# A decoder layer on one Trainium2 core: the routed experts' upper parts in seven block products (Strassen, f32)

## The chip, the cores and the metric

The kernel is one program on one core of a Trainium2 chip. TensorE (PE in the profile, with its weight loads as PEld), VectorE (DVE), ScalarE (ACT), GpSimd (POOL) and SyncE (SP, which here only issues transfers) run their own instruction streams and wait for each other by semaphores. The metric is the device time of one execution in microseconds; a kernel's time is the median of its runs.

## The reference, cut to what matters

The input `x` is 4 x 512 tokens of width 512, in f32. Three sublayers are added to it, each on a layer-normalised copy: causal attention with 32 query and 8 key heads of width 64; a product with a context matrix, both sides rounded block by block to an 8-bit float format; and a mixture of experts. In the last, which the change is about, each token goes to the expert of its highest router score, at most 256 tokens to one expert, and a shared expert takes all tokens:

```python
xd = jnp.zeros((E * C, d), x.dtype).at[flat].set(xt, mode='drop')
xd = xd.reshape(E, C, d)                       # E = 8, C = 256, d = 512
h = jax.nn.silu(jnp.einsum('ecd,edh->ech', xd, W1)) * jnp.einsum('ecd,edh->ech', xd, W3)   # h = 704
oe = jnp.einsum('ech,ehd->ecd', h, W2).reshape(E * C, d)
out = jnp.take(oe, jnp.minimum(flat, E * C - 1), axis=0)
out = out * (gate * keep.astype(x.dtype))[:, None]
shared = jax.nn.silu(xt @ sw1) * (xt @ sw3) @ sw2
return (out + shared).reshape(b, sl, d)
```

The kernel computes these products in f32.

## The kernel before, in words

**Stages.** The attention stage goes through 80 steps written out by hand (`steps`), each with scores, transposes of the probabilities and weighted sums of two or three units. Between them a filler (`Fill.upto`) puts in pieces of other work, kept as generators (`job_q`, `job_k`, `job_v`, `job_o`, the layer norms, the quantised product `job_t`, the router `job_w`). Each job is added with a step from which it may start, a cost in PE time and the jobs that it needs; a job that needs VectorE or GpSimd waits until the filler's own count of GpSimd time (`work.gpsimd`, raised by the helper `gpsimd`) allows it. The result is a fixed order of instructions on every engine. The filler's counts decide places only; they are not hardware.

**Router.** `job_w(b)` normalises block b (512 tokens), computes router scores and places, and scatters the rows to `xd` with four indirect transfers from GpSimd, each waiting for the one before.

**Shared expert.** When the steps are done, `units` take over: `shared_up(b, c)` computes chunk c (128 of the 704 hidden columns) of the upper part for block b, and `shared_down(b, j)` the down product for two tiles of 128 tokens. Between pieces of a unit, `between` lets the filler finish its jobs. A chunk's plain form (`up`) is eight PE products, four over the depth for W1 and four for W3, then Silu on ScalarE and a product on VectorE; the sixth chunk is half W1, half W3 (64 columns each). In blocks 1 to 3 the five full chunks are done by `up7` instead: W1's and W3's columns, stacked, times the block's tokens are one product of a 2 x 2 block matrix with a 2 x 2 block matrix (split by depth and by token half), and Strassen's scheme in Winograd's form needs seven block products for it in place of eight. Each has half the token columns and half the depth, so two PE products. The seven need sums of weight blocks (`weight_sums`, four GpSimd operations a chunk, into `wS` and partly in place) and of token blocks (`token_sums`, four GpSimd operations a block, into `xSs`). The seven results, in PSUM banks, are added up as they come: `p1` and `p5` are copied out by ScalarE, `u2` and `u3` made by VectorE, two more sums (`u2 + p5`, `c2`) by GpSimd, the rest by VectorE; at last GpSimd multiplies the gated half `g` by `c2`.

**Banks.** PSUM banks go by tag: four `sp`, one `av`, three `mm`. `up7` takes six from `sp` and `p5`'s from `av`; the down products of the experts use `mm`.

**Routed experts.** After the jobs, for each of eight experts: `load_rows` brings its 256 rows, `turn_rows` transposes them, `expert_up` calls the plain `up` with 256 columns for six chunks, `down` multiplies by W2, and the rows go to `oe`. The gated chunks lie in what was `wS` (two halves, one for each parity of e). The weights of expert e + 2 take the slot of expert e (`slots[e % 2]`): `load_e(e + 2)` is called after expert e's down product and issues W1, W3 and W2 from SP. The order on PE of one turn of the loop is: chunks 1 and 2 of e, transposes of e + 1, chunks 3 to 5, chunk 0 of e + 1, the down product of e.

**End.** In the last turn `rows_back` brings back 16 tiles of partial results (shared part and residual), ten of them into buffers no longer needed: block 3's `h3x`, `xSs` and the free half of `wS`. Three shared down products are kept for last; beside them GpSimd gathers the experts' rows (16 indirect transfers), VectorE scales and adds them, SP stores the result.

Of the kernel before, what the change touches and what calls it, by code (L numbers as in the profile page):

```python
# [23 lines left out]
def decoder_layer(  # L24
# [18 lines left out]
    nc = tc.nc  # L43
    B, T, D = x.shape
    HD = 64
    NQ = wq.shape[1] // HD
    E, _, H = W1.shape
# [224 lines left out]
    def gpsimd(us, *args):  # L272
        nc.gpsimd.tensor_tensor(*args)  # L273
        work.gpsimd = max(work.gpsimd, work.at) + 1000 * us
# [469 lines left out]
    def add(due, cost, key, gen, *after, want=None):  # L744

        jobs.append(Job(due, cost, key, gen, after, want))

    MM4 = 4 * 860
    for b in range(B):
# [58 lines left out]
        for j in range(TB):  # L808
# [4 lines left out]
        add(ze + 5, 4 * 440 + 4000, ("w", b), job_w(b), *[(("t", b, j), 1) for j in range(TB)], *([(("cs", b + 1), 0)] if b < B - 1 else []))  # L813
    add(8, 0, ("zero",), job_zero())
    jobs.sort(key=lambda x: x.rank())
    for key in [("h", 0)]:
# [267 lines left out]
    def load_ffn(slot, w1, w3, w2, issue, cuts=(0, H)):  # L1084

        v13 = slot[:, 0 : 2 * KC * H].rearrange("p (k h) -> p k h", k=KC)
        v2 = slot[:, 2 * KC * H :].rearrange("p (c d) -> p c d", c=NHC)
        w1r, w3r = (w.rearrange("(k p) h -> p k h", p=P) for w in (w1, w3))  # L1090
        for lo, hi in zip(cuts, cuts[1:]):
            issue(out=v13[:, :, lo:hi], in_=w1r[:, :, lo:hi])
            yield v13, v2
            top = min(hi, H - HT)
            issue(out=v13[:, :, H + HT + lo : H + HT + top], in_=w3r[:, :, lo:top])
            if hi == H:
                issue(out=v13[:, :, H : H + HT], in_=w3r[:, :, top:H])
# [134 lines left out]

    T2 = T // 2
    wS = gp.tile([P, 3, 2, HF * P], F32, name="wS")
    xSs = gp.tile([P, 4, 2, T2], F32, name="xS")
    xS = {}

    def blocks(c):  # L1240

        w, cols = se["w"][0], slice(c * P, (c + 1) * P)
        low = slice(H + HT + c * P, H + HT + (c + 1) * P)
        return w[:, 0:2, cols], w[:, 2:4, cols], w[:, 0:2, low], w[:, 2:4, low]

    def weight_sums(c):

        a11, a12, a21, a22 = blocks(c)
        s2, s3, s4 = (wS[:, i, :, c * P : (c + 1) * P] for i in range(3))
# [5 lines left out]
    def token_sums(b):  # L1255

        x = h3x[b]
        b11, b12, b21, b22 = (x[:, k : k + 2, t : t + T2] for k in (0, 2) for t in (0, T2))
        t1, t2, t3, t4 = (xSs[:, i] for i in range(4))
        gpsimd(1.27, t1, b12, b11, ALU.subtract)  # L1260
        gpsimd(1.27, t3, b22, b12, ALU.subtract)
        gpsimd(1.27, t2, b22, t1, ALU.subtract)
        gpsimd(1.27, t4, b21, t2, ALU.subtract)
        xS[b] = t1, t2, t3, t4, b11, b21, b22

    def up7(b, c, mid):
        a11, a12, s1, a22 = blocks(c)
        s2, s3, s4 = (wS[:, i, :, c * P : (c + 1) * P] for i in range(3))
        t1, t2, t3, t4, b11, b21, b22 = xS[b]

        def product(i, w, x):
            ps = bank("av" if i == 3 else "sp", f"p7_{b}_{c}_{i}")[:, 0:T2]
            for k in range(2):
                nc.tensor.matmul(ps, w[:, k, :], x[:, k, :], start=k == 0, stop=k == 1)  # L1274
            return ps

        def part(tag, bufs=2):
            return gp.tile([P, T2], F32, tag=tag, bufs=bufs, name=f"{tag}_{b}_{c}")

        g = gTs[b][:, c, :]  # L1280
        p1, p5, u2, u3 = part("p1"), part("p5", 1), part("u2"), part("u3")
        c2 = gp.tile([P, T], F32, tag="c2", bufs=2, name=f"c2_{b}_{c}")
        nc.scalar.copy(p1, product(0, a11, b11))
        nc.vector.tensor_tensor(u2, product(1, s2, t2), p1, ALU.add)
        nc.vector.tensor_tensor(u3, product(2, s3, t3), u2, ALU.add)
        if mid:
            mid(2500, 1.3)
        nc.scalar.copy(p5, product(3, s1, t1))
        gpsimd(0.66, u2, u2, p5, ALU.add)
        gpsimd(0.66, c2[:, T2:T], u3, p5, ALU.add)  # L1290
        nc.vector.tensor_tensor(g[:, 0:T2], product(4, a12, b21), p1, ALU.add)
        nc.scalar.activation(g[:, 0:T2], g[:, 0:T2], AF.Silu)
        if mid:
            mid(1700)
        nc.vector.tensor_tensor(g[:, T2:T], product(5, s4, b22), u2, ALU.add)
        nc.scalar.activation(g[:, T2:T], g[:, T2:T], AF.Silu)
        nc.vector.tensor_tensor(c2[:, 0:T2], product(6, a22, t4), u3, ALU.add)
        gpsimd(1.27, g, g, c2, ALU.mult)
        if mid:
            mid(1700, 1.0)  # L1300

    def shared_up(b, c, mid=None):
        if b not in gTs:
            gTs[b] = gp.tile([P, NHC, T], F32, tag="gT", bufs=2, name=f"gT_{b}")
        if b and c < HF:
            up7(b, c, mid)
        else:
            up(se["w"][0], h3x[b], gTs[b], c, T, f"s{b}_{c}", mid)
        if not b and c < HF:
            weight_sums(c)  # L1310
        if c == (HF - 1 if b else HF):
            se["next"] = b + 2
            load_h3(b + 2)
# [10 lines left out]
    def shared_down(b, j, mid=None):  # L1324
        for i in range(b * TB + j, b * TB + j + 2):
            xtile(i)
        for k, py in enumerate(down(gTs[b], se["w"][1], j, f"ys_{b}_{j}", "sp", mid)):
            i = b * TB + j + k
            nc.vector.tensor_tensor(xts[i], py, xts[i], ALU.add)
            if i in routed:  # L1330
                nc.sync.dma_start(out=outf[i * P : (i + 1) * P, :], in_=xts[i])
            elif i not in kept:
                nc.sync.dma_start(out=x2[i * P : (i + 1) * P, :], in_=xts[i])
        if j == 0 and b < B - 1:
            token_sums(b + 1)

    kept = set()
    units = []
# [23 lines left out]
    ctx.enter_context(c_e)  # L1362
    slots.append(ep.tile([P, WSLOT], F32, name="slot_e1"))

    def load_e(e):
        if e < E:
            for evw[e] in load_ffn(slots[e % 2], W1[e], W3[e], W2[e], nc.sync.dma_start):
                pass


    xes, xTs, egTs = {}, {}, {}
    wS_flat = wS.rearrange("p i k c -> p (i k c)")

    def load_rows(e):
        if e < E:
            for t in range(CT):
                xe = ep.tile([P, D], F32, tag="xe", bufs=4, name=f"xe_{e}_{t}")
                r0 = e * CAP + t * P
                nc.sync.dma_start(out=xe, in_=xd[r0 : r0 + P, :])
                xes[e, t] = xe  # L1380
# [9 lines left out]
                    transpose4(xes[e, t], f"ptr_e_{e}_{t}"),  # L1390
                )

    def expert_up(e, c):
        if e < E:
            if c == 0:
                lo = e % 2 * NHC * CAP
                egTs[e] = wS_flat[:, lo : lo + NHC * CAP].rearrange("p (c t) -> p c t", c=NHC)
            up(evw[e][0], xTs[e], egTs[e], c, CAP, f"e{e}_{c}")

    load_rows(0)  # L1400
    load_e(1)
    load_rows(1)


# [1 line left out]
    downs = [u for u in units if u[0] is shared_down]  # L1406
    units = [u for u in ups if u[2] == HF] + downs[:-3] + [u for u in ups if u[2] < HF]
    for i, (f, *args) in enumerate(units):
        if i == len(units) - 1:
            turn_rows(0)  # L1410
        rows_ahead(units[i + 1 :])
        f(*args)
    expert_up(0, 0)


    units = downs[-3:]
# [13 lines left out]
            xtile(i)  # L1430

    for e in range(E):
        for c in range(1, NHC):
            expert_up(e, c)
            if c == 2:
                turn_rows(e + 1)
                load_rows(e + 2)
        expert_up(e + 1, 0)
        if e == E - 1:
            rows_back()  # L1440
        for t, py in enumerate(down(egTs[e], evw[e][1], 0, f"epy_{e}", "mm")):
# [99 lines left out]
```

## Time and profile before

| what | value |
|---|---|
| median of three runs | 1594.07 us (1592.9, 1594.07, 1597.47) |
| the profiled execution's own time | 1587.93 us |
| its span in the profile | 1586.2 us, 20493 instructions |
| PE busy | 1545.7 us, 97% |
| VectorE, ScalarE, GpSimd busy | 849.8, 529.5, 405.1 us |
| attention stage, by PE's timeline | up to some 1085 us |
| shared expert's units | 1085 to 1314 us |
| routed experts | 1314 to 1551 us |
| the kept shared down products and gathers | 1551 us to the end |

The page of a profile shows one execution. A row of a group gives engine, operation, what it writes and reads (buffer numbers left out), shapes and count; a timeline row gives the start, the length over all instructions merged into it, and in brackets the idle time before it with what ended that. An f32 product appears as two matmul records, a f32 transpose as one. A record's length on PE includes the time in which its last columns drain, so the distance of two starts, not the length, tells the pace. `p` is a bank of `up7`, `p_s` one of the shared `up`, `p_e` one of the routed, `epy` and `ys` are banks of the routed and the shared down products, `slot_e` and `slot_s` the weight slots, `ptr_e` the transposes of an expert's rows. All of GpSimd's elementwise work has the helper's line 273.

### The profile page before, as it was taken

To read this page: it belongs to the slowest core of one execution; us is meant where nothing else is said; L and a number is where in the kernel's file an instruction comes from. 1 tells how busy PE (TensorE), PEld (TensorE's weight loads), DVE (VectorE), ACT (ScalarE), POOL (GpSimd) and SP (SyncE) were. 2 spreads that over 40 slices of the span, in tenths; PEclk is the share of its full clock that TensorE was granted. 3 is DMA by queue.
4 is the path that set the end of the run, shared out by engine and by line. 5 is a ranking of instruction groups with operands and counts; after the bars stand their busy time and mean duration, and the time that the engine had idled before them with its cause. 6 is when DMAs were issued, how large, how long until landed. Compare 5 with 4: busy or idle time off the path is not lost.

```text
span 1586.2 us, 20493 instructions
## 1 busy us (share of the span) xinstructions
PE 1545.7 (97%) x6839; PEld 888.4 (56%) x6844; DVE 849.8 (54%) x2459; ACT 529.5 (33%) x1586; POOL 405.1 (26%) x370
## 2 busy tenths in 40 slices
PE   9999999999999999999999999999999999999998
PEld 5555555555544554555555545555455867776773
DVE  4465843458756566787656575665665431111114
ACT  2344453434444433443444444552111321110100
POOL 2021310303343031334312133143365340000004
PEclk9999999999999999999999999999999999999999
DMA  4474431524325253432525342256150350654646
GB/s 140 130 229 134 100 101 47 140 92 102 101 61 151 75 133 101 127 91 69 147 80 144 117 100 61 60 159 187 40 186 27 103 190 19 222 196 139 224 148 225
DMA packets 118346, 194.31 MB, mean 123 GB/s; under 512 B 17120, under 2 KB 36576, under 8 KB 117728
## 3 DMA queue, kind: packets, MB, share of 16 engines
q10 hardware_dynamic: 65472, 100.94, 22.7%
q1 hardware_dynamic: 50208, 83.67, 17.3%
q0 software_dynamic: 2560, 8.39, 1.6%
q8 instruction: 54, 0.88, 0.2%
q14 instruction: 52, 0.43, 0.1%
HBM read 135.54 MB, written 28.05 MB: 103 GB/s over the span
## 4 chain that ended last, share of the span: by engine, by line
PE 84%; DVE 5%; DMA 5%; POOL 2%; ACT 2%; issue 2%; SPq 1%; ACTq 0%; POOLq 0%; DVEq 0%
PE py L408 13%; PE psq L308 12%; PE p_e L1184 10%; PE sc L939 8%; PE av L1020 8%; PE pt L989 7%; PE p L1274 5%; PE epy L1212 4%; PE psv L350 4%; PE ys L1212 3%; PE psk L308 3%; PE p_s L1184 2%; DMA rrb<-rrd 1%; ACT pm L972 1%; PE ptr_h L257 1%
## 5 line engine op out<-in xcount | busy, mean ns | idle before, releaser
L972 ACT ACTIVATE pm<-pm,mn 128x256 f32<-128x256 f32 (+3 forms) x512 | 281.0, 550 | 381.5 <-DVE mn L962 352.5
L962 DVE CUSTOM_DVE_ANT_0 pm<-sc,mask 128x256 f32<-128x256 f32 (+3 forms) x512 | 216.8, 485 | 83.9 <-PE sc L939 83.6
L408 PE MATMUL py<-wo,aT 128*128 128x512 f32 x512 | 238.1, 599 | 1.5 <-issue 0.9
L308 PE MATMUL psq<-hT,wq 128*128 128x512 f32 x512 | 237.6, 601 | 1.7 <-DVE y L604 1.6
L273 POOL TENSOR_TENSOR t1q<-t1q,tsq 128x512 f32<-128x512 f32 x64 | 82.9, 1296 | 395.4 <-DMA tsq<-t2q 193.9
L939 PE MATMUL sc<-kT,t1q 64*128 64x384 f32 (+3 forms) x1024 | 169.2, 450 | 10.8 <-DVE pT L1006 3.5
L1006 DVE COPY pT<-pt 128x128 f32<-128x128 f32 (+3 forms) x256 | 114.0, 484 | 113.6 <-PE pt L989 106.0
L989 PEld LDWEIGHTS pt<-ident,pm 128*128 128x128 f32 x1280 | 145.0, 142 | 39.7 <-issue 28.7
L989 PE MATMUL pt<-ident,pm 128*128 128x128 f32 x1280 | 156.2, 275 | 4.1 <-DVE mn L962 4.0
L1184 PE MATMUL p_e<-h3x,slot_e 128*128 128x256 f32 x704 | 155.1, 380 | 0.0
L1020 PE MATMUL av<-pT,v 128*64 128x512 f32 (+3 forms) x1024 | 152.3, 439 | 1.2 <-ACT pT L1000 1.2
L308 PEld LDWEIGHTS psq<-hT,wq 128*128 128x128 f32 x512 | 92.3, 191 | 102.2 <-issue 97.7
L1000 ACT COPY pT<-pt 128x128 f32<-128x128 f32 (+3 forms) x256 | 96.9, 431 | 155.6 <-PE pt L989 123.6
L408 PEld LDWEIGHTS py<-wo,aT 128*128 128x128 f32 x512 | 92.1, 190 | 96.3 <-issue 88.6
L1184 PEld LDWEIGHTS p_e<-h3x,slot_e 128*128 128x128 f32 x704 | 132.6, 190 | 22.8 <-issue 5.3
L939 PEld LDWEIGHTS sc<-kT,t1q 64*128 64x128 f32 x1024 | 85.4, 186 | 94.3 <-issue 61.2
L1020 PEld LDWEIGHTS av<-pT,v 128*64 128x64 f32 x1024 | 68.3, 136 | 107.7 <-issue 95.6
L273 POOL TENSOR_TENSOR acc<-acc,y 128x512 f32<-128x512 f32 x64 | 81.0, 1270 | 136.1 <-DVE y L604 104.2
L972 ACT ACTIVATION_READ_ACCUMULATOR pm<-pm,mn 128x1 f32 x512 | 95.6, 187 | 0.0
L273 POOL TENSOR_TENSOR aT<-aT,rrb 128x512 f32<-128x512 f32 x64 | 82.0, 1311 | 18.6 <-DMA rrb<-rrd 9.7
L1196 DVE TENSOR_TENSOR wS<-p_e,wS 128x256 f32<-128x256 f32 x40 | 17.0, 424 | 119.3 <-PE p_e L1184 119.3
L1455 POOL DMA_INDIRECT slot_e<-oe,gidx x16 | 15.9, 996 | 243.7 <-DMA oe<-yo 239.1
(201 smaller groups left out, 1690.2 us busy)
## 6 DMA issues: line engine op xcount, KB each, us to landing
slot_e<-in_L_ffn_W_dram SPq DMA_DIRECT2D x14, 1280.0 KB, 12.3
wq<-in_L_attn_wq_dram ACTq DMA_DIRECT2D x16, 1024.0 KB, 6.4
tsq<-t2q SPq DMA_DIRECT2D x256, 64.0 KB, 2.3
wo<-in_L_attn_wo_dram ACTq DMA_DIRECT2D x16, 1024.0 KB, 5.6
rrb<-rrd ACTq DMA_DIRECT2D x32, 512.0 KB, 7.4
slot_e<-in_L_ffn_W_dram SPq DMA_DIRECT2D x7, 1408.0 KB, 6.7
kT<-t1k ACTq DMA_DIRECT2D x64, 128.0 KB, 2.9
wv<-in_L_attn_wv_dram ACTq DMA_DIRECT2D x4, 1024.0 KB, 6.1
```

What stands on the lines that cost most here:

```text
L273: nc.gpsimd.tensor_tensor(*args)
L308: nc.tensor.matmul(ps, w[:, k, c0 : c0 + P], hTs[b][:, k, :], start=(k == 0), stop=(k == KC - 1),)
L408: nc.tensor.matmul(py, aT[:, r, j * P : (j + 1) * P], wts["o", a][:, r, :], start=(r == 0), stop=(r == 3),)
L939: nc.tensor.matmul(scs[g][:, o : o + nk], qTs[b, p][g * HD : (g + 1) * HD, it * P : nk], kTs[b, p // 2][g * HD : (g + 1) * HD, 0:nk], star ...
L962: nc.vector.tensor_tensor_reduce(out=pm[:, o : o + nk], in0=scs[g][:, o : o + nk], in1=mask[:, T - nk : T], scale=-(HD**-0.5), scalar=3.0e ...
L972: nc.scalar.activation(pm[:, o : o + nk], pm[:, o : o + nk], AF.Exp, bias=mn, scale=-1.0, accum_out=rss[b, a][:, col : col + 1],)
L989: nc.tensor.transpose(pt[:, j * P : (j + 1) * P], pms[g][:, j * P : (j + 1) * P], ident)
L1000: nc.scalar.copy(pT[:, 0 : it + 1, it * P : nk], pt[:, o : o + nk].rearrange("p (j t) -> p j t", t=P),)
L1006: nc.vector.tensor_copy(pT[:, it + 1, 0:nk], pt[:, o : o + nk])
L1020: nc.tensor.matmul(av[g * HD : (g + 1) * HD, j * P : T], vs[b][:, j, v0 : v0 + HD], rhs, start=(j == 0), stop=(j == TB - 1),)
L1184: nc.tensor.matmul(pp[:, 0:cols], w13[:, k, o : o + P], xT[:, k, 0:cols], start=(k == 0), stop=(k == KC - 1),)
L1212: nc.tensor.matmul(py, gT[:, c, (t + i) * P : (t + i + 1) * P], w2[:, c, :], start=(c == 0), stop=False,)
```

## The change

- The five full chunks of each routed expert go through `up7` as well, with 256 token columns, so products of 128 columns; the sixth chunk stays as it was and is called before its predecessor's down product (`expert_rest`).
- `weight_sums` of expert e + 1 are made on GpSimd after each chunk of expert e, into the same `wS`, column block by column block; those of expert 0 after each of the last block's shared chunks. `expert_sums(e + 1)`, the four token sums, come after the third chunk. The gated chunks move to the shared expert's W1/W3 slot.
- `load_e(e + 2)` asks for W1 and W3 before the down product of e, `load_w2(e + 2)` for W2 after it.
- In `up7`, for shared and routed alike, the two sums with `p5` move from GpSimd to VectorE and read the bank, so that ScalarE no longer copies `p5` out. For the routed, one Silu covers all columns.
- Token sums: those of block 1 are made after the third chunk of block 0 (before: after its first down unit); of block 3's four, three go to VectorE.
- `job_w` may start four steps later.
- For expert 0, rows are transposed one unit earlier.

```diff
-        add(ze + 5, 4 * 440 + 4000, ("w", b), job_w(b), *[(("t", b, j), 1) for j in range(TB)], ...)
+        add(ze + 9, 4 * 440 + 4000, ("w", b), job_w(b), *[(("t", b, j), 1) for j in range(TB)], ...)
...
+    def token_sums(x, ts, cols, vector=False):
+        half = cols // 2
+        b11, b12, b21, b22 = (x[:, k : k + 2, t : t + half] for k in (0, 2) for t in (0, half))
+        t1, t2, t3, t4 = ts
+        us = 1.27 * cols / T
+        gpsimd(us, t3, b22, b12, ALU.subtract)
+        for out, y, z in (t1, b12, b11), (t2, b22, t1), (t4, b21, t2):
+            if vector:
+                nc.vector.tensor_tensor(out, y, z, ALU.subtract)
+            else:
+                gpsimd(us, out, y, z, ALU.subtract)
...
-        nc.scalar.copy(p5, product(3, s1, t1))
-        gpsimd(0.66, u2, u2, p5, ALU.add)
-        gpsimd(0.66, c2[:, T2:T], u3, p5, ALU.add)
-        nc.vector.tensor_tensor(g[:, 0:T2], product(4, a12, b21), p1, ALU.add)
-        nc.scalar.activation(g[:, 0:T2], g[:, 0:T2], AF.Silu)
+        p5 = product(3, s1, t1)
+        nc.vector.tensor_tensor(u2, p5, u2, ALU.add)
+        nc.vector.tensor_tensor(c2[:, half:cols], p5, u3, ALU.add)
+        nc.vector.tensor_tensor(g[:, 0:half], product(4, a12, b21), p1, ALU.add)
+        if cols == T:
+            nc.scalar.activation(g[:, 0:half], g[:, 0:half], AF.Silu)
...
-        nc.vector.tensor_tensor(g[:, T2:T], product(5, s4, b22), u2, ALU.add)
-        nc.scalar.activation(g[:, T2:T], g[:, T2:T], AF.Silu)
-        nc.vector.tensor_tensor(c2[:, 0:T2], product(6, a22, t4), u3, ALU.add)
-        gpsimd(1.27, g, g, c2, ALU.mult)
+        nc.vector.tensor_tensor(g[:, half:cols], product(5, s4, b22), u2, ALU.add)
+        lo = half if cols == T else 0
+        nc.scalar.activation(g[:, lo:cols], g[:, lo:cols], AF.Silu)
+        nc.vector.tensor_tensor(c2[:, 0:half], product(6, a22, t4), u3, ALU.add)
+        gpsimd(1.27 * cols / T, g, g, c2[:, 0:cols], ALU.mult)
...
+    def expert_sums(e):
+        if e < E:
+            if e:
+                ts = [xSs[:, i, :, e % 2 * P : (e % 2 + 1) * P] for i in range(4)]
+            else:
+                ts = [ep.tile([P, D], F32, tag="yo", bufs=2, name=f"eS_{i}") for i in range(2)]
...
+            exS[e] = token_sums(xTs[e], ts, CAP)
+
+    def expert_rest(e):
+        if e < E:
+            lo = e % 2 * NHC * CAP
+            egTs[e] = egs[:, lo : lo + NHC * CAP].rearrange("p (c t) -> p c t", c=NHC)
+            up(evw[e][0], xTs[e], egTs[e], HF, CAP, f"e{e}_{HF}")
...
     for e in range(E):
-        for c in range(1, NHC):
-            expert_up(e, c)
-            if c == 2:
+        for c in range(HF):
+            up7(evw[e][0], exS[e], egTs[e][:, c, :], c, CAP, f"e{e}_{c}")
+            if e < E - 1:
+                weight_sums(evw[e + 1][0], c)
+            if c == 1:
                 turn_rows(e + 1)
                 load_rows(e + 2)
-        expert_up(e + 1, 0)
+            if c == 2:
+                expert_sums(e + 1)
+        expert_rest(e + 1)
+        load_e(e + 2)
         if e == E - 1:
             rows_back()
         for t, py in enumerate(down(egTs[e], evw[e][1], 0, f"epy_{e}", "mm")):
             yo = ep.tile([P, D], F32, tag="yo", bufs=2, name=f"yo_{e}_{t}")
             nc.vector.tensor_copy(yo, py)
             r0 = e * CAP + t * P
             nc.sync.dma_start(out=oe[r0 : r0 + P, :], in_=yo)
-        load_e(e + 2)
+        load_w2(e + 2)
```

More of the change, by code (lines that the diff above doesn't have):

```diff
@@ L812, in decoder_layer @@
             )
-        add(ze + 5, 4 * 440 + 4000, ("w", b), job_w(b), *[(("t", b, j), 1) for j in range(TB)], *([(("cs", b + 1), 0)] if b < B - 1 else []))
+        add(ze + 9, 4 * 440 + 4000, ("w", b), job_w(b), *[(("t", b, j), 1) for j in range(TB)], *([(("cs", b + 1), 0)] if b < B - 1 else []))
     add(8, 0, ("zero",), job_zero())
@@ L1229, in down, with blocks, weight_sums @@
         return pys
-    T2 = T // 2
     wS = gp.tile([P, 3, 2, HF * P], F32, name="wS")
-    xSs = gp.tile([P, 4, 2, T2], F32, name="xS")
+    xSs = gp.tile([P, 4, 2, T // 2], F32, name="xS")
     xS = {}
-    def blocks(c):
-        w, cols = se["w"][0], slice(c * P, (c + 1) * P)
+    def blocks(w, c):
+        cols = slice(c * P, (c + 1) * P)
         low = slice(H + HT + c * P, H + HT + (c + 1) * P)
[L1244 to L1249, printed above, removed]
+        return (
+            w[:, 0:2, cols], w[:, 2:4, cols], w[:, 0:2, low], w[:, 2:4, low],
+            *(wS[:, i, :, cols] for i in range(3)),
+        )
+    def weight_sums(w, c):
+        a11, a12, a21, a22, s2, s3, s4 = blocks(w, c)
         gpsimd(0.66, s3, a11, a21, ALU.subtract)
@@ L1253, in weight_sums, with shared_sums, up7 @@
         gpsimd(0.66, s4, a12, s2, ALU.subtract)
[L1255 to L1269, printed above, removed]
+    def token_sums(x, ts, cols, vector=False):
[9 more added lines that the diff above has]
+                gpsimd(us, out, y, z, ALU.subtract)
+        return t1, t2, t3, t4, b11, b21, b22
+    def shared_sums(b):
+        xS[b] = token_sums(h3x[b], [xSs[:, i] for i in range(4)], T, b == B - 1)
+    def up7(w, sums, g, c, cols, name, mid=None):
+        a11, a12, s1, a22, s2, s3, s4 = blocks(w, c)
+        t1, t2, t3, t4, b11, b21, b22 = sums
+        half = cols // 2
         def product(i, w, x):
-            ps = bank("av" if i == 3 else "sp", f"p7_{b}_{c}_{i}")[:, 0:T2]
+            ps = bank("av" if i == 3 else "sp", f"p7_{name}_{i}")[:, 0:half]
             for k in range(2):
@@ L1275, in product, with part @@
             return ps
[L1277 to L1283, printed above, removed]
+        def part(tag, n=T // 2):
+            return gp.tile([P, n], F32, tag=tag, bufs=2, name=f"{tag}_{name}")
+        p1, u2, u3, c2 = part("p1"), part("u2"), part("u3"), part("c2", T)
+        nc.scalar.copy(p1[:, 0:half], product(0, a11, b11))
+        p1, u2, u3 = p1[:, 0:half], u2[:, 0:half], u3[:, 0:half]
         nc.vector.tensor_tensor(u2, product(1, s2, t2), p1, ALU.add)
@@ L1305, in shared_up @@
         if b and c < HF:
-            up7(b, c, mid)
+            up7(se["w"][0], xS[b], gTs[b][:, c, :], c, T, f"s{b}_{c}", mid)
         else:
@@ L1309, in shared_up @@
         if not b and c < HF:
-            weight_sums(c)
+            weight_sums(se["w"][0], c)
+            if c == 2:
+                shared_sums(1)
         if c == (HF - 1 if b else HF):
@@ L1333, in shared_down @@
                 nc.sync.dma_start(out=x2[i * P : (i + 1) * P, :], in_=xts[i])
-        if j == 0 and b < B - 1:
-            token_sums(b + 1)
+        if j == 0 and 0 < b < B - 1:
+            shared_sums(b + 1)
     kept = set()
@@ L1363, in decoder_layer, with load_w2 @@
     slots.append(ep.tile([P, WSLOT], F32, name="slot_e1"))
+    loads = {}
     def load_e(e):
         if e < E:
-            for evw[e] in load_ffn(slots[e % 2], W1[e], W3[e], W2[e], nc.sync.dma_start):
-                pass
-    xes, xTs, egTs = {}, {}, {}
+            loads[e] = load_ffn(slots[e % 2], W1[e], W3[e], W2[e], nc.sync.dma_start)
+            for _ in range(2):
+                evw[e] = next(loads[e])
+    def load_w2(e):
+        if e < E:
+            next(loads[e])
+    xes, xTs, egTs, exS = {}, {}, {}, {}
+    egs = se["w"][0].rearrange("p k h -> p (k h)")
     wS_flat = wS.rearrange("p i k c -> p (i k c)")
@@ L1391, in turn_rows @@
                 )
-    def expert_up(e, c):
+    def expert_sums(e):
         if e < E:
[L1395 to L1398, printed above, removed]
+            if e:
+                ts = [xSs[:, i, :, e % 2 * P : (e % 2 + 1) * P] for i in range(4)]
+            else:
+                ts = [ep.tile([P, D], F32, tag="yo", bufs=2, name=f"eS_{i}") for i in range(2)]
+                ts = [t[:, h : h + 2 * P].rearrange("p (k t) -> p k t", k=2) for t in ts for h in (0, 2 * P)]
+            exS[e] = token_sums(xTs[e], ts, CAP)
[4 more added lines that the diff above has]
+            up(evw[e][0], xTs[e], egTs[e], HF, CAP, f"e{e}_{HF}")
     load_rows(0)
     load_e(1)
+    load_w2(1)
     load_rows(1)
@@ L1408, in decoder_layer @@
     for i, (f, *args) in enumerate(units):
-        if i == len(units) - 1:
+        if i == len(units) - 2:
             turn_rows(0)
+            expert_sums(0)
         rows_ahead(units[i + 1 :])
         f(*args)
-    expert_up(0, 0)
+        if f is shared_up and args[1] < HF:
+            weight_sums(evw[0][0], args[1])
+    expert_rest(0)
     units = downs[-3:]
@@ L1432, in decoder_layer @@
     for e in range(E):
-        for c in range(1, NHC):
-            expert_up(e, c)
-            if c == 2:
+        for c in range(HF):
[3 more added lines that the diff above has]
+            if c == 1:
                 turn_rows(e + 1)
                 load_rows(e + 2)
-        expert_up(e + 1, 0)
+            if c == 2:
+                expert_sums(e + 1)
+        expert_rest(e + 1)
+        load_e(e + 2)
         if e == E - 1:
```

## The prediction

> **What bounds the kernel now.** I read the page's busy table and slices first, then the routed experts' stage in a table of windows, then the timelines of PE and POOL.
>
> ```profile
> PE 1545.7 (97%) x6839; PEld 888.4 (56%) x6844; DVE 849.8 (54%) x2459; ACT 529.5 (33%) x1586; POOL 405.1 (26%) x370
> ...
> PE   9999999999999999999999999999999999999998
> ...
> POOL 2021310303343031334312133143365340000004
> ```
>
> PE is busy in all slices; POOL has nothing to do in the six slices before the last, 1309 to 1547 us, which is the experts' stage. One whole expert there (columns: PE, PEld, DVE, ACT, POOL busy, clock, DMA share, GB/s), and PE's own timeline through it (start, length, operation):
>
> ```profile
> 1376.60:1406.30 29.70, 29.70 (x124) 21.57 (x120) 4.00 (x9) 3.37 (x8) 0.00 (x0) 1.00 0.56 186
> ```
>
> ```profile
> 1347.39 7.17 PE L1184 MATMUL p_e<-h3x,slot_e 128*128 128x256 f32 x32
> 1354.40 1.04 PE L257 MATMUL ptr_e<-ident,xe 128*128 128x128 f32 x8
> 1355.28 12.25 PE L1184 MATMUL p_e<-h3x,slot_e 128*128 128x256 f32 x56
> 1367.36 8.75 PE L1212 MATMUL epy<-slot_e,wS 128*128 128x512 f32 x20
> 1376.04 1.13 PE L1222 MATMUL epy<-slot_e,wS 64*128 64x512 f32 x4
> ```
>
> An expert lasts 29.7 us, all of it PE: no other engine ends a wait. A record's length holds its drain, so I take starts. Each f32 product appears as two passes. 256 columns: (7.17-0.38)/31 = 0.219, and over the longer row (1367.36-1355.28)/56 = 0.216 us a pass. The down rows run 0.429 us a pass (8.58/20). The transposes, 128 columns with new weights each time, start (1355.28-1354.40)/8 = 0.11 us apart. Weights reloaded for products of only 8 columns (router scores, on PEld's timeline) show the load's own pace, (0.86-0.19)/6 = 0.11 us:
>
> ```profile
> 540.76 0.86 PEld L655 LDWEIGHTS plg<-wg_sb,h3T 128*128 128x128 f32 x7 [0.24 <-issue]
> ```
>
> **What the Trainium skill says.** "TensorE: Matmul & The Clock Gate", LDWEIGHTS (loading the stationary operand), puts a load at columns/1.2 ns, 107 for 128; the trace shows 0.11 us, agreeing, and the same for a pass of 128 columns, though nothing shows real f32 products of 128 columns on 128 rows. The same page, Architectural detail, calls GpSimd's queue a strict FIFO; the blocked bank sums below agree. "SBUF — State Buffer", Who interferes with whom: a VectorE instruction with at most one SBUF input does not contend with GpSimd, one with two does. The trace agrees: beside two-input VectorE work at 1103 us two GpSimd sums took 1.17 and 1.06 us, elsewhere 0.72.
>
> **Part by part.**
>
> *Products.* An expert's five full chunks took 8 products of 256 columns, 16 x 0.216 = 3.46 us a chunk. Now 7 x 2 of 128 columns, 28 passes. I take 0.112 (load and stream side by side): 3.14 us. Saved: 0.32 x 40 chunks = 12.8 us, all on PE's path. Bounds: 0.1095 a pass gives 15.7; 0.1235 gives nothing; one after the other (0.22) would cost 108.
>
> *GpSimd's new work.* Four weight sums a chunk, for the next expert, and one product g x c2. The pace of such sums:
>
> ```profile
> 1143.36 0.72 POOL L273 TENSOR_TENSOR wS<-slot_s 128x256 f32<-128x256 f32 x1
> 1144.16 0.73 POOL L273 TENSOR_TENSOR slot_s<-slot_s 128x256 f32<-128x256 f32 x1
> 1144.97 0.73 POOL L273 TENSOR_TENSOR wS<-slot_s 128x256 f32<-128x256 f32 x1
> 1145.78 0.72 POOL L273 TENSOR_TENSOR wS<-slot_s,wS 128x256 f32<-128x256 f32 x1
> ```
>
> Starts are 0.80 apart where one feeds the next, 0.69 otherwise: 3 x 0.80 + 0.69 = 3.1 us a chunk, 0.7 for the product: 3.8, against PE's 3.14. So GpSimd falls behind. Count from an expert's first pass. Chunk 0's product can start at 3.8 (3.14, then about 0.65 through VectorE, Silu and semaphores). Then 0.7 + 3.1 for each of chunks 0, 1, 2, the next expert's four token sums (0.69 + 0.80 + 0.80 + 0.69 = 3.0), 0.7 + 3.1 for chunk 3, 0.7 for chunk 4: 3.8 + 11.4 + 3.0 + 3.8 + 0.7 = 22.7 us. PE meanwhile does 15.7 of products, 0.9 of transposes, the next expert's rest chunk (8 x 0.216 = 1.7), and in the down product reaches chunk 4 after 8 x 0.429 = 3.4: 21.7. It waits 1.0 us there, the other down passes behind it. Seven experts prepare a next one: +7.0 us. The queue is empty again at 25.8, before the next chunk 0. If the sums take 4% longer, 0.8 us more a time.
>
> *VectorE, ScalarE.* Seven 128-column operations at about 0.29 us (the 64x128 rows took 0.29) and their gaps are 2.1-2.5 us a chunk, ScalarE 0.27 + 0.38: both beside 3.14 of PE. The four score banks return 0.7 us or more before their reuse. I count zero. Without that cover, 40 chunks x 0.2 = 8 us.
>
> *Weights and buffers.* The gated rows of the experts move from the bank of weight sums to the shared experts' weight slot, free by then: zero. W1 and W3 are asked for once the up part's last read is done, W2 after the down part. 2.9 MB at the 371-388 GB/s of the loads is 7.8 us; landed near 27 us, first summed at 33. Zero; SP carries as many issues as before, and the later output stores wait on transfers long landed.
>
> *Bank sums on VectorE, shared experts.* In block 3 now:
>
> ```profile
> 1279.33 1.01 POOL L719 DMA_INDIRECT xd<-h,r_dst_i  x1 [4.12 <-DVE r_flat L715]
> 1282.72 0.96 POOL L719 DMA_INDIRECT xd<-h,r_dst_i  x1 [2.38 <-DMA xd<-h,r_dst_i]
> 1285.69 0.96 POOL L719 DMA_INDIRECT xd<-h,r_dst_i  x1 [2.01 <-DMA xd<-h,r_dst_i]
> 1288.68 0.96 POOL L719 DMA_INDIRECT xd<-h,r_dst_i  x1 [2.02 <-DMA xd<-h,r_dst_i]
> 1289.66 0.73 POOL L273 TENSOR_TENSOR u<-u,p 128x256 f32<-128x256 f32 x1
> ```
>
> ```profile
> 1290.91 1.13 PE L1274 MATMUL p<-xS,wS 128*128 128x256 f32 x4 [3.13 <-DVE gT L1295]
> ```
>
> Four scatters, each waiting for the one before, hold GpSimd for 10.3 us; the sums u and c2 stood behind them, VectorE behind u, PE behind VectorE: 3.1 us. On VectorE they need no GpSimd. What is late next: block 3's token sum t3, now behind the scatters, about 0.9 us after PE wants it (built order: the scatters start some 9 us before the block's first product). Net -2.3 (bounds -3.1, +1). Against it 2 more VectorE operations of 0.42 us in 15 chunks, 12.6 us, VectorE about half busy there; where layer-norm chains stand ahead, PE waits: +0.8 (0 to 3).
>
> *Routers put back* by four units: same instructions, other places in the attention stage; PE's stalls there move. Nothing prices it: 0, bounds -4, +4.
>
> *End.* Ten rows read back into free buffers were spread over the last expert; six of them and six more reads wait now for its last up product, 12 x 0.26 MB, about 9 us in flight when the last expert rows are stored: gathers 0.4 us later. The chain ends on them: +0.5 (0 to 2).
>
> Sum: -12.8 + 7.0 - 2.3 + 0.8 + 0 + 0.5 = **-6.8 us**. The profiled execution took 1587.93 (span 1586.2); it would take 1581.1. It stands 6.1 under the median of the three, 1594.07, to which I carry the difference: **1587.3**.
>
> **Rivals.**
>
> *GpSimd hides wholly* (no wait for chunk 4): -13.8, 1580.3. For it: an expert's GpSimd work, 5 x 3.8 + 3.0 = 22 us, fits in 28. Against: the last product's place in the queue.
>
> *GpSimd becomes the bound, slower.* If the sums meet VectorE as at 1103 us, each gains 0.39 us. The 24 operations ahead of chunk 4's product decide it: 2 long ones an expert undo the experts' gain, 5 (+1.95 x 7 = 13.7) make 1601, ten 1614.5. For: the long sums are the same instruction. Against: every VectorE operation of the new stage reads one operand from PSUM; beside those u and c2 took 0.73.
>
> *Passes of 128 columns don't overlap their loads.* At 0.13 a pass 28 x 0.13 x 40 = 145.6 stands against 138.2 before, and GpSimd is then hidden: +7.4 - 2.3 + 0.8 + 0.5 = +6.4, 1600.5. At 0.19 (a load's whole record) 1668. Against: both 0.11 rows.
>
> *The attention stage pays it back:* stalls of 1-3 us move the wrong way by 4 with VectorE's 3: 1593.5, no change.
>
> **How the numbers follow.** 0.3%, 4.8 us, is about what a measurement here can tell from no change. Forecast 0.47 and hidden GpSimd 0.11 are faster, 0.58. Paid back 0.24: same. GpSimd the bound 0.14, passes not overlapping 0.04: slower 0.18. The range runs from hidden GpSimd with attention's gain (1576) to five long sums (1601); the forecast's own is 1582 to 1592, from the bounds of its small terms.
>
> **What would show it.** Passes of 128 columns starting 0.11 apart; the first-half down product waiting about 1 us in every expert but the last, its releaser POOL; POOL busy some 20 us an expert; a period near 29.1; no 3 us wait in block 3. Wrong if a pass exceeds 0.12, if sums run over 0.8, or if waits of VectorE's appear inside chunks.

## The result, and the profile after

| | median | runs | ratio to before |
|---|---|---|---|
| before | 1595.25 us | 1592.9 to 1597.47 | |
| after | 1571.16 us | 1569.79 to 1572.75 | 0.985, 95% interval 0.9831 to 0.9868 |

The change gives 24 us, where 6.8 was forecast; 1571.16 lies below the range, which began at 1576. The profiled execution took 1569.79 us, 18.1 less than that of before. The busy table and two rows of the slices after the change:

```profile
PE 1530.8 (98%) x7324; PEld 890.5 (57%) x7324; DVE 920.8 (59%) x2732; ACT 535.1 (34%) x1611; POOL 546.0 (35%) x569
...
PE   9999999999999999999999999999999999999998
...
POOL 2022301203334121334313133143445147776744
```

GpSimd now works in the slices that were empty, the experts' stage. One expert there, in the table of windows (stretch, length, PE, PEld, DVE, ACT, POOL busy, clock, DMA share, GB/s):

```profile
1360.00:1389.10 29.10, 28.25 (x182) 21.87 (x182) 11.26 (x39) 4.77 (x13) 20.60 (x29) 1.00 0.57 191
```

PE's timeline shows where the missing 0.85 us is: the passes run without a gap, and the down product stops after 8 of its passes until GpSimd has written the fifth gated chunk.

```profile
1347.86 0.61 PE L1281 MATMUL p_e<-xS,slot_e 128*128 128x128 f32 x4
1348.30 1.89 PE L1184 MATMUL p_e<-h3x,slot_e 128*128 128x256 f32 x8
1350.03 3.60 PE L1212 MATMUL epy<-slot_e,slot_s 128*128 128x512 f32 x8
1354.44 5.42 PE L1212 MATMUL epy<-slot_e,slot_s 128*128 128x512 f32 x12 [0.82 <-POOL slot_s L273]
```

(1348.30 - 1347.86)/4 = 0.11 us a pass of 128 columns. The passes before the stop take 8 x 0.429 = 3.43 us from 1350.03, so the next was due at 1353.46 and came 0.98 late (the record subtracts the drain and says 0.82). GpSimd's timeline agrees: the fifth product, the last of these rows, comes directly after the four weight sums of the chunk before.

```profile
1350.58 0.73 POOL L273 TENSOR_TENSOR wS<-slot_e 128x256 f32<-128x256 f32 x1
1351.38 0.72 POOL L273 TENSOR_TENSOR slot_e<-slot_e 128x256 f32<-128x256 f32 x1
1352.18 0.72 POOL L273 TENSOR_TENSOR wS<-slot_e 128x256 f32<-128x256 f32 x1
1352.99 0.72 POOL L273 TENSOR_TENSOR wS<-slot_e,wS 128x256 f32<-128x256 f32 x1
1353.67 0.72 POOL L273 TENSOR_TENSOR slot_s<-slot_s,c_e 128x256 f32<-128x256 f32 x1
```

So the experts went as forecast. **Where the time came from** is seen by comparing the two traces at four marks:

| stage (mark on PE) | before, us | after, us | difference |
|---|---|---|---|
| start to the last `av` | 1085.1 | 1073.3 | -11.8 |
| to the first `epy` | 252.6 | 247.6 | -5.0 |
| to the last `epy` | 212.8 | 210.7 | -2.1 |
| to the end | 35.7 | 36.5 | +0.8 |

The attention stage, costed at nothing, gave 11.8 of the 18.1 us. (The middle rows shift work between them: the chunk that stands before the first `epy` for the second expert is now the half-size rest chunk, 1.73 us shorter, which the third row then lacks as a saving. Put right, they are -3.3 and -3.8; of the -3.3, 1.6 are the first expert's own products.) PE's idle time between 380 and 1085 us is 20.6 us before and 12.5 after. PE's waits in that stretch (line, releaser: total, times, longest), before:

```profile
PE pt L989 <- DVE mn L962: 4.0, 3, 3.3
PE sc L939 <- issue: 2.5, 1, 2.5
PE sc L939 <- DVE pT L1006: 2.3, 3, 1.4
```

and after:

```profile
PE psq L308 <- DVE y L604: 2.3, 3, 1.0
PE py L408 <- issue: 2.0, 1, 2.0
PE av L1020 <- ACT pT L1000: 1.7, 1, 1.7
...
PE sc L939 <- DVE pT L1006: 0.8, 2, 0.4
```

The longest of before, on PE's timeline and on VectorE's:

```profile
625.86 2.37 PE L1020 MATMUL av<-pT,v 128*64 128x512 f32 x16
631.51 3.37 PE L989 MATMUL pt<-ident,pm 128*128 128x128 f32 x16 [3.27 <-DVE mn L962]
```

```profile
624.61 0.16 DVE L238 TENSOR_SCALAR veb<-mvb 128x4 f32<-128x4 f32 x1
...
625.87 1.26 DVE L245 TENSOR_TENSOR r0b<-veb,rsb 128x4 f32<-128x4 f32 x1
...
628.14 0.69 DVE L317 TENSOR_TENSOR t2q<-psq,rt 128x512 f32<-128x512 f32 x1
628.75 0.68 DVE L319 TENSOR_TENSOR t1q<-psq,rt 128x512 f32<-128x512 f32 x1
629.35 0.34 DVE L368 RECIPROCAL rr<-rs 128x32 f32<-128x32 f32 x1
629.61 0.45 DVE L251 TENSOR_SCALAR h<-acc,mvb,rsb 128x512 f32<-128x512 f32 x1
630.09 0.69 DVE L460 TENSOR_REDUCE am<-h 128x4 f32<-128x512 f32 x1
630.69 0.28 DVE L962 CUSTOM_DVE_ANT_0 pm<-sc,mask 128x128 f32<-128x128 f32 x1
```

A layer norm's inverse root, 13 tiny operations from 624.61 to 628.12 (3.5 us), and five operations after it (2.6 us) stand in VectorE's queue ahead of the mask-and-minimum operations (L962). One of the 13 took 1.26 us where its like took 0.16; GpSimd had an operation of the same 1.26 us from 625.86. ScalarE's exponentials wait for the L962 operations, the transposes `pt` for ScalarE, and between `av` and `pt` the filler had put nothing on PE. After the change the same chain stands behind those operations, where PE has other work:

```profile
626.63 0.08 DVE L962 DVE_READ_ACCUMULATOR2_ANT mn<- 128x1 f32 x1
627.14 1.56 DVE L1006 COPY pT<-pt 128x128 f32<-128x128 f32 x3 [0.42 <-PE pt L989]
628.62 0.16 DVE L238 TENSOR_SCALAR veb<-mvb 128x4 f32<-128x4 f32 x1
```

The wait of 3.27 us also cost more than its length: a stretch at half the granted clock (0.5 in the clock records, in place of 1.0) followed it. Four stretches of the kernel before, in the table of windows: the ends of the two longest attention waits, the third wait (1290.91, shown in the prediction), and an undisturbed stretch.

```profile
626.00:636.00 10.00, 6.22 (x35) 4.42 (x34) 9.66 (x30) 4.99 (x17) 3.42 (x3) 0.83 0.22 45
918.00:928.00 10.00, 7.49 (x22) 2.86 (x21) 8.37 (x38) 3.83 (x13) 0.00 (x0) 0.83 0.93 215
...
1286.00:1296.00 10.00, 6.87 (x33) 5.72 (x32) 2.88 (x7) 1.88 (x5) 5.69 (x7) 1.00 0.42 138
1376.60:1386.60 10.00, 10.00 (x52) 8.45 (x49) 2.13 (x4) 1.84 (x4) 0.00 (x0) 1.00 0.79 276
```

0.83 over 10 us is 3.4 us at half clock. In the clock records these windows begin at 631.0 and 924.6, within 0.6 us of the waits' ends, and each loses at most 1.7 us. The kernel after has one such window in its attention stage too, from 354.6 us, behind a wait of 1.46. So of the 11.8 us, 8.1 are idle time that is gone and at most 1.7 are slow clock; the other 2 are not accounted for. Of the 8.1 us, 3.8 are the waits at `pt` (4.0 to 0.2) and 1.1 the one at `sc` released by "issue" (2.5 to 1.4); the rest is smaller waits that went, less some that came.

### The profile page after: what moved, and what is told of

It is laid out like the page before. It is cut to its first block, busy times and chain, and to the rows that moved or that the text cites. A ratio compares the mean times of both kernels' runs of the same rounds, so it can differ in the third digit from the quotient of the medians.

```text
span 1568.1 us, 22176 instructions
## 1 busy us (share of the span) xinstructions
PE 1530.8 (98%) x7324; PEld 890.5 (57%) x7324; DVE 920.8 (59%) x2732; ACT 535.1 (34%) x1611; POOL 546.0 (35%) x569
## 4 chain that ended last, share of the span: by engine, by line
PE 69%; POOL 8%; DVE 2%; DMA 2%; issue 2%; ACT 1%; SPq 0%; ACTq 0%; POOLq 0%; DVEq 0%
PE py L408 12%; PE psq L308 10%; PE sc L939 7%; PE av L1020 7%; PE pt L989 6%; PE p_s L1281 5%; PE p_e L1281 5%; PE epy L1212 3%; PE p_s L1184 3%; PE psv L350 3%; POOL wS L273 3%; PE psk L308 3%; PE ys L1212 2%; POOL xS L273 1%; POOL slot_s L273 1%
## 5 line engine op out<-in xcount | busy, mean ns | idle before, releaser
L962 DVE CUSTOM_DVE_ANT_0 pm<-sc,mask 128x256 f32<-128x256 f32 (+3 forms) x512 | 216.7, 485 | 91.4 <-PE sc L939 91.4
L939 PE MATMUL sc<-kT,t1q 64*128 64x128 f32 (+3 forms) x1024 | 167.0, 451 | 6.8 <-ACT pT L1000 2.5
L1212 PE MATMUL epy<-slot_e,slot_s 128*128 128x512 f32 x160 | 71.8, 597 | 5.8 <-POOL slot_s L273 5.8
L1212 PE MATMUL ys<-slot_s,gT 128*128 128x512 f32 x160 | 71.7, 596 | 0.0
L416 DVE TENSOR_TENSOR acc<-py,acc 128x512 f32<-128x512 f32 x64 | 43.8, 686 | 46.3 <-PE py L408 45.6
L317 DVE TENSOR_TENSOR t2q<-psq,rt 128x512 f32<-128x512 f32 x64 | 44.0, 688 | 43.1 <-PE psq L308 40.2
```

The source lines that it names most:

```text
L939: nc.tensor.matmul(scs[g][:, o : o + nk], qTs[b, p][g * HD : (g + 1) * HD, it * P : nk], kTs[b, p // 2][g * HD : (g + 1) * HD, 0:nk], star ...
L962: nc.vector.tensor_tensor_reduce(out=pm[:, o : o + nk], in0=scs[g][:, o : o + nk], in1=mask[:, T - nk : T], scale=-(HD**-0.5), scalar=3.0e ...
L1212: nc.tensor.matmul(py, gT[:, c, (t + i) * P : (t + i + 1) * P], w2[:, c, :], start=(c == 0), stop=False,)
```

## The experiments

All ratios are to runs of the kernel before on the same chip; intervals are 95%. R is the move of the routers, S the change in the shared experts, E the routed experts.

| run | what it has | median, us | ratio | interval |
|---|---|---|---|---|
| router_only | R | 1580.76 | 0.9915 | 0.9898 to 0.9932 |
| pace_only | R's effect on pacing alone | 1581.29 | 0.9923 | 0.9898 to 0.9948 |
| place_only | R's place alone | 1595.53 | 1.0015 | 1.0004 to 1.0027 |
| banks_only | S, bank sums alone | 1595.76 | 1.0003 | 0.999 to 1.0017 |
| shared_only | S | 1590.74 | 0.9971 | 0.9955 to 0.9986 |
| experts_only | E (its bank sums too) | 1591.23 | 0.9988 | 0.9975 to 1.0001 |
| after_router5 | S + E | 1583.22 | 0.9935 | 0.9918 to 0.9951 |
| shared_router | R + S | 1576.41 | 0.9875 | 0.9859 to 0.9892 |
| after | R + S + E | 1571.16 | 0.985 | 0.9831 to 0.9868 |
| tokens_vector | all, other token sums | 1569.62 | 0.983 | 0.9814 to 0.9846 |
| sums_late | all, one chunk's sums later | 1564.21 | 0.9814 | 0.9797 to 0.983 |
| late_t3 | sums_late, `t3` on VectorE | 1561.91 | 0.9808 | 0.978 to 0.9836 |
| long_wait | all, longer waits of PE | 1590.51 | 0.9983 | 0.9973 to 0.9993 |

**The routers alone, and all but the routers.**

```diff
 router_only (to the kernel before)
-        add(ze + 5, 4 * 440 + 4000, ("w", b), job_w(b), ...)
+        add(ze + 9, 4 * 440 + 4000, ("w", b), job_w(b), ...)
 after_router5 (to the kernel after): the same line back to ze + 5
```

> The kernel before with one edit: job_w may start, and is ranked, at ze + 9 instead of ze + 5. Theory: this alone makes the attention stage some 11.5 us shorter (the kernel after reaches the end of the attention stage 11.9 us earlier in the trace), so about 1583 us against 1595, ratio 0.993; the PE waits of 3.3 us at 631 us and 2.5 us at 924 us are gone. Rival: the attention stage differs from execution to execution or through the other edits: within 3 us of the kernel before.

> The kernel after with job_w put to ze + 5 again: all else of the change, without the router's move. Theory: about 11.5 us slower than the kernel after, 1582 to 1584 us, ratio to before 0.992 to 0.993, and the experts' stage is as in the kernel after (period 29.16 us). Rival (the gain comes with the bank sums and the experts): 1571 us.

One number in one line is worth 13 us, more than all the rest (some 10.5). The profile of after_router5 has before's waits again (`pt` 3.9 us, `sc` 2.5 us). In that of router_only the former is gone from the head of the list and the latter is down to 1.4 us; its last `av` starts at 1074.6 us, 10.5 before that of the kernel before, and both have two half-clock windows up to there.

**Pace or place.** The number that `add` gets is two things: the step from which the job may start, and its rank. `share` goes through the jobs by rank, adds up the PE time left in them, and sets from that how much filler each step needs so that every projection is done when it is wanted. The two were separated:

```diff
 pace_only (to the kernel before)
-        for job in sorted(todo, key=lambda x: x.rank()):
+        seen = lambda x: x.rank() + (4 if x.key[0] == "w" else 0)
+        for job in sorted(todo, key=seen):
...
-            if job.want > n + 20:
+            if seen(job) > n + 20:
 place_only (to the kernel before): ze + 9 as in router_only, and share with -4 in place of 4
```

> The kernel before; job_w keeps its place in the filler's list (ze + 5), but the function share, which sets how much projection work is put into each step, counts job_w's remaining cost as if it ranked four steps later. Theory: it is the pacing of the projections that the router's rank changes, and with it where VectorE's layer-norm chains fall beside PE work: most of the gain of the router's move, 8 to 13 us, ratio 0.992 to 0.995. Rival (the place of the router's own pieces matters): within 3 us of before.

> The kernel before with job_w ranked at ze + 9, while share counts its cost as at ze + 5: the other half of the router's move. Theory (pacing): within 3 us of before, ratio 0.998 to 1.002. Rival (place): 8 to 13 us less, ratio 0.992 to 0.995.

The place alone gains nothing (1.0015, if anything a little slower), and the pacing alone gives as much as the whole move. The waits agree: place_only still has `pt` 4.0 us and `sc` 2.5 us in the stretch from 380 to 1085 us; pace_only, like router_only, has no `pt` at the head of the list and 1.4 us at `sc`. By the code, a router counted four steps less urgent changes how much filler goes into the steps of the blocks' ends; with it the q, k and o products, and the VectorE operations that they bring, stand elsewhere in the fixed orders. That other values than 9 would do as well was not run.

**The shared experts.**

```diff
 banks_only (to the kernel before; shared_only has this too)
-        nc.scalar.copy(p5, product(3, s1, t1))
-        gpsimd(0.66, u2, u2, p5, ALU.add)
-        gpsimd(0.66, c2[:, T2:T], u3, p5, ALU.add)
+        p5 = product(3, s1, t1)
+        nc.vector.tensor_tensor(u2, p5, u2, ALU.add)
+        nc.vector.tensor_tensor(c2[:, T2:T], p5, u3, ALU.add)
 shared_only: also the change's token sums for blocks 1 and 3
```

> The kernel before with one edit: in the shared experts' up7 the two sums with p5 are made by VectorE from the bank, ScalarE's copy of p5 is gone; routers, token sums and routed experts as before. Theory: the wait of 3.1 us behind the four scatters goes, about 2 us less, 1593, ratio 0.998 to 1.000. Rival: VectorE, more loaded, delays PE inside the chunks by more than that: slower by 1 to 3 us.

> The kernel before with all that the change does in the shared experts and nothing else: bank sums on VectorE, block 1's token sums after the third chunk of block 0, three of block 3's four token sums on VectorE; routers as before, routed experts plain. Bank sums alone gave 1.0003: they took GpSimd's scatters out of the chain of sums, but left the token sums behind the scatters, and block 3 waited 4.8 us. Experts alone gave about 2 us less, all of it without the routers 10.5. Theory A (the two parts need each other: VectorE must have both the bank sums and the token sums): no wait above 2 us at block 3's first products, and 5 to 9 us less than before. Theory B (the experts' part is worth its 6 to 8 us, but was lost behind block 3's wait and the halved clock after it, which is not there any more in the whole): this run is only 2 to 4 us below before. Block 1's wait of 2.7 us stays in both.

Bank sums alone gain nothing: the wait in block 3 changes its cause. PE's waits from 1085 us on, in banks_only:

```profile
PE p L1274 <- POOL xS L273: 4.6, 1, 4.6
```

GpSimd's timeline in banks_only, and below it the same token sums in the kernel before, whose scatters began at 1279.33:

```profile
1273.90 1.01 POOL L719 DMA_INDIRECT xd<-h,r_dst_i  x1 [1.36 <-DVE r_flat L715]
...
1283.48 0.96 POOL L719 DMA_INDIRECT xd<-h,r_dst_i  x1 [2.62 <-DMA xd<-h,r_dst_i]
1284.47 2.48 POOL L273 TENSOR_TENSOR xS<-h3x 128x512 f32<-128x512 f32 x2
1286.91 2.60 POOL L273 TENSOR_TENSOR xS<-h3x,xS 128x512 f32<-128x512 f32 x2
```

```profile
1270.16 2.49 POOL L273 TENSOR_TENSOR xS<-h3x 128x512 f32<-128x512 f32 x2 [2.87 <-DMA h3x<-h3d]
1272.61 2.60 POOL L273 TENSOR_TENSOR xS<-h3x,xS 128x512 f32<-128x512 f32 x2
```

In the kernel before, the four token sums stood ahead of the scatters; in banks_only they stand behind them. The edit itself does not touch either, so the planned order has moved here too. The filler's count of GpSimd time, which the two sums no longer raise, is a likely reason, but it was not tested alone. With three of the token sums on VectorE too, shared_only has 1.3 us left of this wait and is 4.9 us faster than the kernel before (2 to 7 by its interval). The bank sums thus gain only with the token sums; token sums alone were not run. In the whole change one sum, `t3`, is still there, as PE's waits in the shared stage of the kernel after show in their second row:

```profile
PE p_s L1281 <- DVE xt L1339: 2.6, 1, 2.6
PE p_s L1281 <- POOL xS L273: 1.4, 1, 1.4
```

**The routed experts.**

```diff
 experts_only: the kernel after, with ze + 5, and p5 and the shared token sums as before
 shared_router: shared_only with ze + 9
```

> The kernel after with the routed experts' part alone: routers at ze + 5, the shared blocks' sums with p5 on ScalarE and GpSimd as before, all shared token sums on GpSimd at their places of before. Theory (parts add up; bank sums alone gave 1.0003): the experts' stage gives 0.6 us in seven experts and 1.6 in the last, the block 3 wait of 3.2 us stays: 6 to 8 us less than before, 1586 to 1588, ratio 0.995 to 0.996. Rival (bank sums with token sums on VectorE give nothing): as the kernel after with routers put to ze + 5, 1583, ratio 0.9935.

> The kernel of the run before this one with the routers put back by four as well, so the whole change without the routed experts. Beside the whole change (ratio 0.985) it gives the experts' worth where attention and block 3 have no long waits. If the step of the prediction on the experts holds (12.8 saved, 7.0 waited, 0.5 at the end: 5.3), it takes some 5 to 6 us more than the whole; that would be a ratio to before of about 0.9885. If the experts are worth 2 as in the run of them alone, 0.9865; if they are worth over 9, 0.991 or more.

Alone they give 1.9 us, less than expected and not clear of nothing by the interval. Beside shared_router, the whole change has 0.0025 less, 4 us, with an uncertainty of some 4; beside shared_only, after_router5 has 0.0036 less, 5.7 us, again with some 4. The forecast of 5.3 fits the last two, but the times alone don't fix it. In the traces the experts' gain is the same everywhere, 0.55 to 0.67 us a period; experts_only keeps before's wait in block 3 (3.05 us, this time with 6.8 us of half clock), and its first down product waits 1.9 us. That the rest of the difference is the clock fits its mean, 0.9936 against 0.9942 for before, but wasn't isolated.

**GpSimd's queue.**

```diff
 sums_late (to the kernel after; late_t3 has it too)
-            if e < E - 1:
-                weight_sums(evw[e + 1][0], c)
+            if e < E - 1 and c != 3:
+                if c == 4:
+                    weight_sums(evw[e + 1][0], 3)
+                weight_sums(evw[e + 1][0], c)
 late_t3: in token_sums, t3 joins the loop that goes to VectorE for block 3
 tokens_vector (to the kernel after)
-            exS[e] = token_sums(xTs[e], ts, CAP)
+            exS[e] = token_sums(xTs[e], ts, CAP, e > 0)
```

> The kernel after with the weight sums of the fourth chunk moved behind the product g x c2 of the fifth on GpSimd (no work less). Theory: the wait of 1.0 us of the down product in seven experts is GpSimd's queue; it goes, 7 us less than the kernel after, about 1564 us, ratio to before 0.981; the period is 28.2 us. Rival: the wait is for something else (ScalarE's Silu, VectorE's c2), or a wait of the next expert's first chunks takes its place: 1571 us.

> The kernel after with the weight sums of the fourth chunk behind the fifth chunk's product (as in the run that gave 1564.2) and block 3's last token sum t3 moved from GpSimd, where it stands behind the four scatters, to VectorE. Theory: PE's wait of 1.5 us in block 3's first chunk is for t3; it goes, about 1.5 us less, 1562.7, ratio 0.980. Rival: VectorE's sums then meet the scatters' use of GpSimd or come later themselves: 1564 to 1566.

> The whole change, with three of the four token sums of each next expert on VectorE in place of GpSimd. GpSimd's queue is then 2.3 us shorter ahead of the fourth chunk's and the fifth chunk's product, so by the count of the prediction the wait of 1.0 us in the down product of seven experts goes (7 us less than the whole change, about 1564). Rival: the two-input sums on VectorE meet GpSimd's two-input sums and lengthen both (as at 1103 us in the profile of before, 0.4 us each), and VectorE's bank reads come later, so the wait stays or turns up as waits of products for their banks: 1570 or more.

sums_late puts the fifth product ahead of the sums: no expert waits, the period is 28.07 in place of 29.16 us, and 7 us are gained. late_t3 takes the wait in block 3 as well; its 2.3 us more lie within the intervals, its profile has no wait of 0.6 us or more left in that block. These beat both kernels. tokens_vector shortens GpSimd's queue too and gains little: the periods are 28.66 or 29.24. The wait at the down product is gone, and another is there, in the chunk after the token sums:

```profile
PE p_e L1281 <- DVE u_e L1290: 1.6, 3, 0.5
```

The view has 1.6 us of it; from one start of a pass to the next, PE loses 0.6 or 1.2 us an expert. GpSimd's weight sums took 745 ns on average (726 in the kernel after, both from the costliest groups of the stage), and the bank sums `u_e` stand behind three token sums on VectorE: shifted work turned into a wait for a bank.

**Does a wait cost more than its length?**

```diff
 long_wait (to the kernel after), in the loop over c
+            if c == 3 and e < E - 1:
+                for i in range(3):
+                    a11, a12, a21, a22, s2, s3, s4 = blocks(evw[e + 1][0], i)
+                    gpsimd(0.66, s4, a12, s2, ALU.subtract)
```

> The whole change, with three more weight sums on GpSimd (0.72 us each, repeats of s4 of chunks 0 to 2 of the next expert) ahead of the fifth chunk's product in seven experts, so that the wait of 1.0 us in each of the seven down products becomes one of about 3.2 us. It asks whether a wait of PE costs more than its length. Theory A (a wait of about 3 us brings on a window of some 3.4 us at half clock, as stands after the 3 us waits of the kernel before and not after the 1.0 us waits of the changed one): seven more such windows, each 1.7 us, the clock at 0.990 or lower, and 7 x 2.2 + 7 x 1.7 = 27 us more than the whole change, about 1598. Theory B (the windows have nothing to do with waits): 7 x 2.2 = 15 us more, about 1587, clock as before at 0.996 to 0.998.

PE's waits, and the windows after four of the seven, in long_wait:

```profile
PE epy L1212 <- POOL slot_s L273: 20.0, 7, 2.9
```

```profile
1329.00:1334.00 5.00, 4.26 (x7) 2.00 (x8) 0.00 (x0) 0.00 (x0) 3.53 (x6) 0.66 0.26 79
1362.00:1367.00 5.00, 4.58 (x7) 2.03 (x8) 0.00 (x0) 0.00 (x0) 3.21 (x5) 0.66 0.17 45
1394.00:1400.00 6.00, 4.67 (x11) 2.20 (x12) 0.00 (x0) 0.00 (x0) 4.13 (x6) 1.00 0.31 103
...
1457.00:1463.00 6.00, 5.26 (x9) 2.25 (x10) 0.00 (x0) 0.00 (x0) 3.54 (x6) 0.72 0.21 61
```

Each wait grew by 2.05 us to 3.03 (start to start), 14.4 us in all; the time grew by 19.3 (medians) or 21 (ratios). Three of the seven waits brought the half clock in this execution; three windows of up to 1.7 us are about the 5 us that are left. The mean clock of 20 runs fell to 0.9927, from 0.996 to 0.998 in the four of after. So neither all nor none: a chance. The 20 runs spread over 8 us, the four of after over 3. What the chance hangs on is in the last section.

## Why the prediction was wrong, point by point

- **Products, -12.8: right.** In the kernel after the passes are 0.112 us apart on average; with the wait gone (sums_late) an expert is 29.71 - 28.07 = 1.64 us shorter, 13.1 for eight.
- **GpSimd's wait, +7.0: right.** Seven waits of 0.97 to 1.02 us, POOL the releaser, 20.6 us of GpSimd work an expert, period 29.16 (forecast 29.1). sums_late gained 7.
- **Shared experts, -2.3 and +0.8: right in sum, in part by luck.** What is left of the middle stages is -1.7, against -1.5. But of the 3.1 us wait, `t3` kept 1.4 and not 0.9, and no wait for VectorE took its place, so two misses cancel. And the bank sums do not do it alone (1.0003): the step counted `t3` as late and had the other three token sums on VectorE, but did not say that its gain hangs on that.
- **End, +0.5:** 0.8 in the traces.
- **Routers, 0 with bounds of 4 either way: the step that failed.** The attention stage became 11.8 us shorter in the profiled executions (10.5 with the move alone), and the move is worth 13 in the medians. "Same instructions, other places" was true; that the stalls would about cancel had no ground, and the bounds had no source. What the runs showed in its place is the pacing: `share` reads the router's rank, and through it the orders of every engine changed, so that PE's idle time from 380 to 1085 us fell from 20.6 to 12.5 us, with the wait of 3.3 us gone and that of 2.5 shortened to 1.4. The waits view of before had the numbers for a bound: 20.6 us of idle PE, with these two waits at its head; on the gain side the bound was some 20, not 4. And the changed orders could be read: the root chain ahead of L962 in the one, behind it in the other.
- **Carrying the difference to the median: the second, smaller miss.** The profiled execution of before stood 7.3 us under the median of all its runs, that of after 1.4 under. It had drawn few half-clock windows: its mean clock was 0.997, while the 15 runs of before beside router_only had 0.991 at 1599.4 us to 0.996 at 1591.1. Over all 81 runs of before beside the experiments, 0.001 of the clock goes with some 1.3 us. A change that takes waits away also takes some of these windows away. At one clock of 0.996, the six runs of before took 1591.0 to 1593.0 us and two of after 1572.1 on average, which leaves some 20 of the 24 us (the runs are from several chips). "TensorE: Matmul & The Clock Gate" of the Trainium skill bears on this in Part 1: The HAM clock gate: one idle window of about 3.4 us brings the half clock back, and the windows run freely, whatever the kernel does. Its table Why this matters for your kernels advises against PE gaps beyond about 3 us. The prediction drew on that page for loads only. The traces agree on the 3.4 us and on the free run, and are stricter on the gap: see the last section.
- **The rivals.** GpSimd did not become the bound (sums 0.726 us, 0.80 apart), and passes did overlap their loads. The attention stage moved, with the sign opposite to the rival's.

## What to carry to other kernels

In a kernel whose order comes from a planner, a number that only ranks one job can move every engine's order: compare the planned orders at the places of the longest waits before costing it at nothing, and bound it by the idle time of the whole stretch. In these traces a TensorE wait of 2.4 us or more was followed by half clock in 30 of 44 cases, and each window of 3.4 us cost up to 1.7 us beyond the wait, so remove long waits before many short ones. When work is moved off a queue, look at the order in which the rest of that queue is then planned; and when a queue is too long by a little, moving the one late result ahead can gain more than moving work to another engine.

## What the runs showed of the hardware that was not expected

- In the 14 profiled executions, leaving out the first wait of each, a half-clock window followed 30 of 44 PE waits of 2.4 us and more, 11 of 47 of 1.4 to 2.4 us, and 2 of 70 of 0.9 to 1.4 us. It began 1.7 to 4.3 us after the wait's start. The seven waits of 1.0 us in the experts of the kernel after brought none. So a gap clearly under 3 us is enough at times. A window is mostly 3.41 us long, but 6.8 us stand in five of the traces and 10.2 us in one, so the loss can be a multiple of 1.7 us.
- What the chance hangs on can be read from the same traces. In each execution, all half-clock windows begin whole multiples of 3.4133 us apart, to within 3 ns. Cut each execution into stretches of that length on its own grid, leaving out the first 12 and the last 20 us and stretches already at half clock. PE was idle for over 2.05 us in 25 of them, and the next was at half clock every time; with 0.9 to 2.05 us idle it was so in 12 of 126. In long_wait, the stretches that held the most of each of the seven waits had 2.46, 2.35 and 2.10 us idle where half clock followed, and 2.00, 1.75, 1.62 and 1.52 where none did. A wait of 3 us that falls across a border of the grid can so pass free, as the one at 1287.8 to 1290.9 us of the kernel before did. That idle time of one stretch is the cause is a reading of these traces, and no run placed a wait on purpose.
- One VectorE operation that reads one block from SBUF took 3.31 us beside GpSimd, and 0.54 when repeated; the block 1 wait of 2.6 us, in every kernel here, stands behind it. The row, from VectorE's timeline of after:

```profile
1158.33 3.31 DVE L251 TENSOR_SCALAR h<-acc,mvb,rsb 128x512 f32<-128x512 f32 x1
...
1162.27 0.54 DVE L251 TENSOR_SCALAR h<-acc,mvb,rsb 128x512 f32<-128x512 f32 x1
```

  GpSimd had an indirect transfer and two sums one after the other in those 3 us (1157.84 to 1161.34). In all 14 traces, the operations of this form with no GpSimd work beside them took 0.45 to 0.55 us; of those beside it, most took 0.53 to 0.59, so being beside GpSimd is not enough. "SBUF — State Buffer" of the Trainium skill, Who interferes with whom, lists `tensor_scalar` among the operations that can enter a two-port mode and then contend with GpSimd, where the one that issues first blocks the other. The prediction gave that section's rule for one SBUF input without this exception. The length fits, but no run here took GpSimd's work away to show it.
